# Filter matmuls of both frequency units side by side, six set-up buffers, a separate piece order for the ends, and a new order in the full ticks

## Chip, cores, metric

One core of one Trainium2 chip. The metric is the time of one execution in microseconds (us) of device time; medians of 3 to 7 executions. All executions quoted here were in the same (fast) state, at a mean granted TensorE clock of 0.97 to 0.99. The rounds of experiments ran on different chips; the kernel before, timed again in each, gave medians of 5686.9 to 5687.9 us. PE is TensorE's matmul stream, PEld its weight loads, DVE VectorE, ACT ScalarE, POOL GpSimd, SP SyncE (which only issues transfers here).

## The reference, cut to what matters

Two layers of a MetaFormer block on `x` of 8 x 128 x 128 x 96. Per layer and image:

```python
x_pre = soa(einsum('bhwc,mc->bhwm', ln(x), w1))            # 96 -> 192 channels
xf    = rfft2(x_pre)                                       # 128 x 65 frequencies
comb  = einsum('shwm,bsm->bhwm', filt, softmax(gate(x)))   # 3 resized filters, mixed per image
x     = x + einsum('bhwm,cm->bhwc', irfft2(xf * comb), w2)
t     = x.reshape(B, H * W, C)
x     = t + qlinear(relu(qlinear(q(ln(t)), W1)), W2)       # fp8 products, f16 roundings
```

The Fourier transforms are matmuls with constant matrices. The filters are small (48 rows) and are resized on the fly by a matmul with `k_rh`.

## The kernel before, where the change touches it

The kernel runs as three Python generators, cut at each `yield`: `pixels` (P: a group of 8 image rows through normalisation, `w1` and the first transform), `frequencies` (F: 4 of the 65 columns through filter, second transform, product and inverse) and `tokens` (S: last inverse transform and the fp8 network), plus `gate` (G, once per image) and small normalisation steps (N). A table fixes in which order their pieces are issued in one **tick**; F runs 18 groups behind P and S 38 behind. So there are five phases: set-up, pixels only, pixels and frequencies, some 218 full ticks, frequencies and tokens, tokens only.

```python
TICK = (                       # (stage, piece, groups ahead), 70 entries
    ("S", 22, -2), ("G", 0, -1), ("P", 1, 2), ("F", 2, 0), ("S", 2, 2), ("F", 13, -1),
    ("F", 3, 0), ("P", 3, 1), ("G", 1, -1), ("S", 0, 3), ("N", 0, 0), ("P", 5, 0), ...
)
...
        groups = [[(0, 2)], [(2, 2)] + [(4, 1)] * (n > KC)]
        for units in groups:                      # a unit: two columns, 384 channels
            for j, u in units:
                pf = bank2("pf")                  # one of four PSUM tiles
                ...  mm(pf[...], utf[64*i : 64*i+NHS, ...], kt["rh"][64*i : 64*i+NHS, :])  # 12 matmuls, 48 rows
                py = bank2("py")
                ...  mm(py[...], alf[...], kt["fwd"][:, e, :])                             # 12 matmuls, 128 rows
            yield
            ...  nc.scalar.copy(cv, pf[...])      # cf, ACT
            yield
            ...  products pr = py * cf            # DVE
            yield
            ...  xf = pr[0] + pr[1]               # POOL
            yield
...
        for h in range(2):                        # xn_c: 8 fp8 normalisations per token group
            for j in range(RH * h, RH * h + RH):
                if h in NORM_ACT:  nc.scalar.activation(xn[:, j, :], ...)      # NORM_ACT = ()
                else:              nc.vector.tensor_scalar(xn[:, j, :], ...)
            yield
...     # per third k of the network: y (ACT) -> a (DVE) -> h (POOL) ; at the end y = x + o (POOL)
```

Set-up: all constants on SP's queue, then all filters `cw` (8 loads, 3.7 MB) from POOL's queue, then each layer's small loads; then `u_d` (the half-resized filters, 24 tiles of 65 x 8 x 192) is written from a ring of three buffers.

## Time and profile before

| | before |
|---|---|
| median of 3 | 5689.54 us (5685.1 to 5690.01) |
| first pixel transposes (end of set-up) | 120.2 us |
| pixels only, to the first `pf` | 164.4 us |
| pixels and frequencies, to the first `ps_r` | 301.0 us |
| full ticks, to the last `pa` | 4570.8 us |
| frequencies and tokens, to the last `pi` | 303.0 us |
| tokens only and last stores | 224.8 us |

The phases are read from PE's timeline at the first or last record of the tile named. Lines of the profile are shown in the prediction.

### The profile page before, as it was taken

Reading aid. Unit: us, or ns where it says so; the run is one execution under the profiler, and the core shown is the slowest. Engines: PE = TensorE matmul, PEld = TensorE weight load, DVE = VectorE, ACT = ScalarE, POOL = GpSimd, SP = SyncE. Lnnn points to the kernel's source line nnn. Section 1 sums busy time; section 2 is a strip of 40 time slices with the busy share of each in tenths; the row PEclk is TensorE's granted clock in tenths of the full one; section 3 lists DMA queues with packets and bytes.
Section 4 is the critical chain, followed back from the end, with each engine's and each line's share of the span. In section 5 each row is a group of like instructions: output and inputs, shape, how many; then the busy total and the mean of one; then the engine's idle time right before and its main releaser. Section 6 shows DMA issues by size and latency. Waiting matters only on the chain.

```text
span 5684.2 us, 111449 instructions
## 1 busy us (share of the span) xinstructions
PE 5416.2 (95%) x39144; PEld 4252.6 (75%) x39144; DVE 4387.5 (77%) x11780; ACT 3059.9 (54%) x4575; POOL 4063.1 (71%) x6309
## 2 busy tenths in 40 slices
PE   4899999999999999999999999999999999999876
PEld 1687877878787787878778787877878788787753
DVE  3666787787878778787887878778787877778875
ACT  2444555555555555555555555555555555554444
POOL 1565677777777777777777777777777777777876
PEclk9999999999999999999999999999999999999986
DMA  5465767767676676767667676776767677675642
GB/s 140 145 171 151 198 183 189 196 179 195 179 194 187 187 194 176 195 180 196 185 186 195 180 193 180 194 192 181 195 178 195 178 193 196 178 195 161 169 123 94
DMA packets 830267, 1019.78 MB, mean 179 GB/s; under 512 B 54891, under 2 KB 762203, under 8 KB 829371
## 3 DMA queue, kind: packets, MB, share of 16 engines
q1 hardware_dynamic: 829324, 1008.82, 65.6%
q8 instruction: 312, 5.11, 0.4%
q0 software_dynamic: 384, 3.83, 0.3%
q14 instruction: 247, 2.02, 0.1%
HBM read 598.62 MB, written 413.84 MB: 178 GB/s over the span
## 4 chain that ended last, share of the span: by engine, by line
PE 82%; DVE 7%; POOL 5%; issue 1%; ACT 0%; POOLq 0%; DVEq 0%; ACTq 0%
PE pw L404 13%; PE py L544 13%; PE pa L424 11%; PE pf L533 7%; PE pz L605 7%; PE pz L600 6%; PE pi L619 5%; PE ps_r L649 5%; PE pm L691 5%; PE po L708 4%; PE pt_a L393 4%; DVE xn_c L673 2%; PE pt_c L681 2%; POOL h L703 1%; POOL y L722 1%
## 5 line engine op out<-in xcount | busy, mean ns | idle before, releaser
L703 POOL CAST h<-a 128x1024 fp8e5<-128x1024 f16 x768 | 842.3, 1099 | 962.4 <-DVE a L697 958.0
L411 DVE TENSOR_TENSOR xs<-pw,r 128x768 f32<-128x768 f32 x512 | 489.6, 956 | 766.8 <-ACT r L407 766.8
L582 POOL TENSOR_TENSOR xf<-pr 128x768 f32<-128x768 f32 (+2 forms) x544 | 949.7, 1748 | 67.4 <-DVE pr L574 63.3
L404 PE MATMUL pw<-w,xT 97*128 97x240 f32 x4096 | 921.8, 369 | 5.2 <-DVE yt L626 4.4
L544 PE MATMUL py<-k_fwd,al 128*128 128x128 f32 x6272 | 848.2, 284 | 1.5 <-ACT cf L559 1.2
L404 PEld LDWEIGHTS pw<-w,xT 97*128 97x128 f32 x4096 | 759.5, 191 | 85.7 <-DVE yt L626 11.3
L424 PE MATMUL pa<-xs,dft 128*128 128x384 f32 x2048 | 767.1, 497 | 30.9 <-DVE xs L411 19.1
L544 PEld LDWEIGHTS py<-k_fwd,al 128*128 128x128 f32 x6272 | 740.0, 191 | 73.1 <-issue 5.5
L694 ACT CAST y<-pm 128x1024 f16<-128x1024 f32 x768 | 777.6, 1016 | 1.2 <-PE pm L691 1.1
L559 ACT COPY cf<-pf 128x768 f32<-128x768 f32 (+2 forms) x544 | 419.6, 775 | 536.5 <-PE pf L533 521.7
L673 DVE TENSOR_SCALAR xn_c<-xr,n_rs,n_nb 128x96 fp8e5<-128x96 f32 x2048 | 634.4, 378 | 18.0 <-POOL n_nb L355 16.5
L407 ACT ACTIVATE r<-pw 128x960 f32<-128x960 f32 x512 | 497.0, 971 | 280.9 <-PE pw L404 140.9
L570 DVE TENSOR_TENSOR pr<-py,cf 128x768 f32<-128x768 f32 (+2 forms) x544 | 497.5, 915 | 176.0 <-PE py L544 142.9
L533 PEld LDWEIGHTS pf<-k_rh,ut 48*128 48x128 f32 x6272 | 390.5, 186 | 279.2 <-issue 143.5
L600 PE MATMUL pz<-w2b,xf 128*128 128x192 f32 (+1 forms) x2112 | 551.8, 343 | 27.1 <-POOL xf L582 24.0
L424 PEld LDWEIGHTS pa<-xs,dft 128*128 128x128 f32 x2048 | 367.7, 191 | 224.2 <-DVE xs L411 36.2
L533 PE MATMUL pf<-k_rh,ut 48*128 48x128 f32 x6272 | 494.3, 289 | 1.7 <-DVE pr L574 1.7
L615 ACT COPY zt<-pz 128x384 f32<-128x384 f32 x528 | 251.5, 476 | 448.9 <-PE pz L605 448.5
L600 PEld LDWEIGHTS pz<-w2b,xf 128*128 128x128 f32 (+1 forms) x2112 | 341.3, 191 | 190.6 <-issue 77.6
L691 PE MATMUL pm<-xq,f_q 96*128 96x512 fp8e5 x1536 | 475.7, 393 | 7.5 <-ACT o L717 7.4
L396 ACT ACTIVATE xT<-pt_a 96x1024 f32<-96x1024 f32 x256 | 261.4, 1021 | 395.7 <-PE pt_a L393 395.7
L514 POOL TENSOR_TENSOR ut<-ut,rw 112x768 f32<-112x768 f32 (+1 forms) x256 | 471.6, 1842 | 0.0
(125 smaller groups left out, 10386.8 us busy)
## 6 DMA issues: line engine op xcount, KB each, us to landing
a_d<-at SPq DMA_DIRECT2D x256, 768.0 KB
al<-a_d SPq DMA_DIRECT2D x960, 192.0 KB
v<-y_d SPq DMA_DIRECT2D x256, 384.0 KB
y_d<-yt SPq DMA_DIRECT2D x480, 192.0 KB
ut<-u_d SPq DMA_DIRECT2D x240, 336.0 KB
xt<-in_x_dram SPq DMA_DIRECT2D x128, 384.0 KB
xr<-in_x_dram SPq DMA_DIRECT2D x128, 384.0 KB
mid<-y SPq DMA_DIRECT2D x128, 384.0 KB
```

What stands on the lines that cost most here:

```text
L404: mm(o, xT[:, s * RH + i + j, :], wt["w1"], start=True, stop=True)
L407: nc.scalar.activation(r.rearrange("p s j c -> p s (j c)"), pw, AF.Relu)
L424: mm(pa[:, s], wt["dft"], xss[i // 2][:, s], start=True, stop=True)
L533: mm(pf[:nm, i, t * 128 : (t + 1) * 128], utf[64 * i : 64 * i + NHS, c0 : c0 + nm], kt["rh"][64 * i : 64 * i + NHS, :], start=True, stop=True,
L544: mm(py[:nm, t, e, :], alf[:, e, c0 : c0 + nm], kt["fwd"][:, e, :], start=True, stop=True,)
L570: nc.vector.tensor_tensor(p0, yq, crb, ALU.mult)
L582: nc.gpsimd.tensor_tensor(xv[:q, te], pr[:q, 0, te].rearrange("p t r k -> p t (r k)"), pr[:q, 1, te].rearrange("p t r k -> p t (r k)"), AL ...
L600: mm(o[:, : u * C], xf[:kb, 1, e, :], wt["w2b"][:kb, : u * C], start=True, stop=False,)
L673: nc.vector.tensor_scalar(xn[:, j, :], x8[:, j, :], nm.rs[:, 1, j : j + 1], nm.nb[:, 1, j : j + 1], ALU.mult, ALU.add, saturate=False,)
L691: mm(pm[:, s, :], fk, xq[:, s, :], start=True, stop=True)
L694: nc.scalar.copy(y16, pm)
L703: nc.gpsimd.tensor_copy(hk, a16, saturate=False)
```

## The change

Intent: visit the filter matmuls once per tick instead of twice; give the stretches with only pixels or only tokens an order of their own (`SOLO`); take four of eight `xn_c` of the last image from DVE to ACT; spread the gate; let the set-up begin earlier.

```diff
+TAIL_ACT = (1,)
 TICK = (
-    ("S", 22, -2), ("G", 0, -1), ("P", 1, 2), ("F", 2, 0), ("S", 2, 2), ...
+    ("P", 17, -1), ("F", 13, -1), ("F", 14, -1), ("S", 2, 2), ("S", 18, -1), ("F", 2, 0), ...
+    ... ("G", 0, 0) and ("G", 1, 0) late in the tick before, ("G", 2, -1) to ("G", 6, -1) spread
+SOLO = ( ... P, S and N pieces only ... )
-            nc.gpsimd.dma_start(cw[...], p["cw"][...])
+            nc.sync.dma_start(cw[...], p["cw"][...])
-            u = us.tile([NKW, UN, M], F32, name="u", bufs=3)
+            u = us.tile([NKW, UN, M], F32, name="u", bufs=6)
+    constants("dft", "rw")                       # first; the other constants after the filters
+        for l, p in enumerate(layers):
+            wts.append(prepare(us, l, p))        # small loads of a layer, then its filters
+            cws.append(load_filters(us, l, p))
+        constants("fwd", "inv", "idft", "rh", "mask")
-        for units in groups: ... pf, py / cf / products / xf per unit
+        pf0, pf1 = filter_mm(0, 2), filter_mm(2, 2)
+        yield
+        py0 = fft_mm(0, 2)
+        yield
+        cf0, cf1 = filter_out(2, pf0), filter_out(2, pf1)
+        ...                                      # products, xf, py1 (+ the fifth column), products, xf
-                if h in NORM_ACT:
+                if h in NORM_ACT or (h in TAIL_ACT and jb.n == len(jobs) - 1):
+            alone = t < offset["F"] - 2 or t > n + offset["F"]
+            for stage, step, ahead in SOLO if alone else TICK:
```

## The prediction

> **What bounds the kernel now.** I read the page first: busy shares, the 40 slices, the chain of work that ended last.
>
> ```profile
> PE 5416.2 (95%) x39144; PEld 4252.6 (75%) x39144; DVE 4387.5 (77%) x11780; ACT 3059.9 (54%) x4575; POOL 4063.1 (71%) x6309
> PE   4899999999999999999999999999999999999876
> PEclk9999999999999999999999999999999999999986
> PE 82%; DVE 7%; POOL 5%; issue 1%; ACT 0%; POOLq 0%; DVEq 0%; ACTq 0%
> ```
>
> TensorE (PE) sets the pace from slice 2 to slice 36; only the first 2 and the last 3 or 4 slices (142 us each) show PE idle. The whole idle time of PE is 5684 - 5416 = 268 us, so if "busy" meant "useful" there would be little to win in the middle. So I went to the timeline of PE in one steady tick (a tick: one group of pixels, one of frequencies, one of tokens). `ps_r` comes once a tick, so its starts give the period: 1994.34 to 2014.44 is 20.10 us, and 13 of the 16 ticks of an image have just that.
>
> ```profile
> 1994.34 1.48 PE L649 MATMUL ps_r<-v,k_idft 128*128 128x384 f32 x4
> ...
> 2000.56 1.46 PE L619 MATMUL pi<-zt,k_inv 128*128 128x384 f32 x4
> 2001.94 0.94 PE L533 MATMUL pf<-k_rh,ut 48*128 48x128 f32 x12
> 2002.81 1.60 PE L544 MATMUL py<-k_fwd,al 128*128 128x128 f32 x12
> 2004.25 1.18 PE L708 MATMUL po<-f_q,h 128*128 128x96 fp8e5 x24
> ...
> 2014.44 1.48 PE L649 MATMUL ps_r<-v,k_idft 128*128 128x384 f32 x4
> ```
>
> Read starts, not durations (ends are modelled). The 4 `pi` records take 2000.56 to 2001.94 = 1.38 us, though records of that width follow each other every 0.322 us (4 x 0.322 = 1.29): 0.09 lost before `pf`. The 12 `pf` records take 0.87; in the narrowed timeline they start in pairs 0.112 apart, so 6 x 0.112 = 0.67: 0.20 lost, half at the first pair and half after the last. The 12 `py` take 1.44 against 12 x 0.112 = 1.34: 0.10 lost at the first. One visit to the filter matmuls so costs 0.09 + 0.20 + 0.10 = **0.39 us of PE time counted as busy**, twice a tick. The weight-load row shows the same hole, idle just before the visit:
>
> ```profile
> 2001.94 0.75 PEld L533 LDWEIGHTS pf<-k_rh,ut 48*128 48x128 f32 x12 [0.55 <-ACT n_std L343]
> ```
>
> Adding up the other departures from each record's usual spacing in that tick gives 0.4 us, so a steady tick is PE-issue-bound with almost no waits. The exceptions are the two ticks per image with the gate:
>
> ```profile
> 1821.45 1.48 PE L649 MATMUL ps_r<-v,k_idft 128*128 128x384 f32 x4
> ...
> 1833.70 0.90 PE L465 MATMUL pl<-fc,hb 36*112 36x384 f32 x2 [1.29 <-DVE xs L411]
> ...
> 1835.71 1.65 PE L708 MATMUL po<-f_q,h 128*128 128x96 fp8e5 x24 [0.79 <-ACT lg L470]
> ...
> 1845.93 1.53 PE L424 MATMUL pa<-xs,dft 128*128 128x384 f32 x4 [0.97 <-DVE xs L411]
> ...
> 1848.81 1.48 PE L649 MATMUL ps_r<-v,k_idft 128*128 128x384 f32 x4
> ...
> 1873.42 1.48 PE L649 MATMUL ps_r<-v,k_idft 128*128 128x384 f32 x4
> ```
>
> They last 27.36 and 24.61 us, 11.8 above two plain ticks. Some 4 us of that are real PE work (gate matmuls, the fifth column of the last frequency group); from the spacings I count 5.7 us of waits on VectorE (DVE), which has 11 us of gate arithmetic there. Outside the full ticks, three stretches where PE waits:
>
> ```profile
> 204.88 3.18 PE L424 MATMUL pa<-xs,dft 128*128 128x384 f32 x8 [0.48 <-DVE xs L411]
> 5230.50 0.59 PE L600 MATMUL pz<-w2b,xf 128*128 128x192 f32 x2 [1.69 <-POOL xf L582]
> L703 POOL CAST h<-a 128x1024 fp8e5<-128x1024 f16 x46 | 49.9, 1101 | 34.4 <-DVE a L697 33.2
> ```
>
> They are a pixels-only tick (period 8.03, 1.3 of it waits), a tick of frequencies and tokens alone (mean 15.95 us, PE waits for GpSimd's `xf`), and the tokens-only end (period 10.93; GpSimd itself sits idle 2.2 us per tick for `a`, clock granted 0.67).
>
> **What the Trainium skill says.** "TensorEngine Tiling (Array Packing)", Key Properties: "Changing tiling mode (not just tile) drains the TensorE". `pf` alone in the steady tick contracts over 48 rows in two row groups; everything else uses the full height. The trace agrees, with 0.39 us per visit. "TensorE: Matmul & The Clock Gate", Part 2 step 1: weight loads are pulled ahead of running matmuls; it agrees, loads run ahead everywhere but at these borders. "Trainium Kernel Development and Optimization", Reading a trace, calls matmul busy time a bad metric: agreed, the drain hides inside a PE that is 99% busy between 2000 and 3000 us. "DMA: Bandwidth & Descriptors", on why a DMA increments its semaphore by 16: a transfer is spread over the largest number of engines up to 16 that divides its slowest dimension; 65 partitions give 13 of 16, 81%. The trace agrees: while the `u` tiles are written (56 to 104 us) the DMA share is 0.78 at 212 GB/s.
>
> **The change part by part.** The counts of instructions on all engines stay, except that 64 normalisations go from DVE to ACT and 8 filter loads from GpSimd's to SyncE's queue.
>
> 1. *Filter matmuls together.* Both units' `pf` now stand back to back, then `py`. One visit less in each of 256 frequency ticks (the last group of an image goes from 3 visits to 2). 256 x 0.39 = 100 us; of these 238 ticks are PE-bound now (the other 18 are in item 5): **93 us**. The cost is that two PSUM tiles of four are held at once. I followed the slots through the new order by hand: `pf` takes slots freed by the last `pm` and by `ps_r`; `py1` needs the slot that the first products free, some 1.7 us ahead; `pw1` to `xs` to `pa1` has some 1.4 us. No wait should appear. A plain tick: 20.10 - 0.39 = 19.7, perhaps 19.5.
>
> 2. *Gate in the full ticks.* Gate steps 0 and 1 move into the tick before, the rest is spread. DVE's 16 us per tick plus the 11 are still more than one tick holds, so not all waits go: I take 3 of 5.7, times 15 images: **45 us**.
>
> 3. *Own order for pixels only.* `pw` of the next group now stands between the two `pa`, so `xs` has time. PE floor by spacing: `pt_a` 8 x 0.109, `pw` 16 x 0.202, `pa` 8 x 0.322, together 6.7 us; I take 6.8. 17 ticks x (8.03 - 6.8) = **21 us**.
>
> 4. *Set-up.* First pixel transposes at 120 us. The `u` and padding writes, 24 x 390 KB + 2 x 780 KB = 10.9 MB at 212 GB/s, are 51 us and already fill the 13 engines, so **six buffers alone should give nothing**. But the first write leaves at 55.8; the constants and the first layer's small loads stood behind 3.7 MB of filters (one issue took 16.55 us). In the new order the issues alone (about 0.5 us each, some 60) end near 36 us. First write near 38: **17 us**.
>
> 5. *Frequencies and tokens alone.* The new tick puts both `pf` and the first products early, so `xf` is ready sooner. GpSimd then bounds: 3 casts x 1.1, 2 `xf` x 1.81, `ut` 1.82, `y` 1.64, and 12 small norms x 0.28: 13.7 us. I take 14.3 of 15.95: 17 x 1.6 = **27 us**.
>
> 6. *Tokens only.* GpSimd again: 3.3 + 1.64 + 3.4 = 8.3 us of work per 10.93. With the new order and four normalisations per tick on ACT (about 6 us busy, an estimate from its rows) I take 8.9: 17 x 2.0 = **34 us**.
>
> Sum: 93 + 45 + 21 + 17 + 27 + 34 = 237 us; 5689.5 - 237 = 5452, say 5450.
>
> **The rivals.** *PSUM pressure takes it back:* two `pf` held until ACT has read both leave two slots, and a steady tick gets a new wait of 0.4 us or more. For: four slots, in-order engines, DVE at 80% in the tick. Against: the hand count above. It would leave about 5540. *DVE becomes the bound in the gate ticks:* two such ticks hold 43 us of DVE work against 44 of PE; if the new place only moves the waits, item 2 is zero and the time 5495. *The drain does not disappear with grouping,* because each switch between row groups costs it: against it, pairs inside `pf` already alternate 7 ns apart; it would give 5545. *Only the ends gain:* items 3 to 6 alone, 5590. *Better than thought:* all gate waits go, tick 19.5, end ticks at their floors: 5380.
>
> **Range and chances.** Item 1 is the surest and alone about 1.6%; items 2, 5 and 6 (106 us) I hold to within half. So 5395 to 5510. Under 2% needs over half of the sum to fail (over 5576): faster 0.95, same 0.04, slower 0.01.
>
> **What would show it.** The period of `ps_r` at 19.7 or a little less, and one visit to `pf` of 24 records per tick, with its lost 0.39 once; the two gate ticks together near 48 us instead of 52; pixels-only period 6.8; tokens-only 8.9 with GpSimd's wait for `a` gone; first transposes near 103 us with the same 212 GB/s while `u` is written. It is wrong if the tick stays at 20.1, or `pf`, `py1` or `pa` show idle time before them in a plain tick.

## The result and the profile after

**5454.01 us** (5453.05 to 5458.97, 4 runs) against 5689.77 of before: ratio 0.9589, 95% interval 0.9572 to 0.9606. Ratios here are the mean time of one kernel's fast runs over that of the other's of the same rounds, so not quite the ratio of the medians quoted. The sum of the prediction held, but its terms did not all hold:

| phase | before | after | won | predicted (items) |
|---|---|---|---|---|
| set-up | 120.2 | 115.4 | 4.8 | 17 (4) |
| pixels only | 164.4 | 136.5 | 27.9 | 21 (3) |
| pixels and frequencies, and full ticks | 4871.8 | 4696.3 | 175.5 | 138 (1, 2) |
| frequencies and tokens | 303.0 | 295.9 | 7.1 | 27 (5) |
| tokens only and last stores | 224.8 | 208.1 | 16.7 | 34 (6) |

The profile page of the kernel after: busy shares and the chain that ended last.

```profile
PE 5231.9 (96%) x39144; PEld 4283.1 (79%) x39144; DVE 4371.0 (80%) x11716; ACT 3081.5 (57%) x4639; POOL 4168.3 (76%) x6301
PE 86%; POOL 5%; DVE 4%; DMA 2%; issue 2%; ACT 1%; SPq 1%; POOLq 0%; DVEq 0%; ACTq 0%
```

PE's "busy" fell by 184 us with the same 39144 matmuls, so that much of it had not been needed for them (the grouping alone, the second run below, takes 67 us of it: 5349.3 busy). The share rose by one point only, so the share does not show it. A steady tick, PE's timeline after (start, duration, engine, line, tile):

```profile
1875.82 1.45 PE L686 MATMUL ps_r<-v,k_idft 128*128 128x384 f32 x4
1877.11 0.49 PE L637 MATMUL pz<-w2b,xf 128*128 128x192 f32 x2
...
1878.72 1.61 PE L553 MATMUL pf<-k_rh,ut 48*128 48x128 f32 x24
1880.26 1.60 PE L566 MATMUL py<-k_fwd,al 128*128 128x128 f32 x12
...
1884.19 1.46 PE L656 MATMUL pi<-zt,k_inv 128*128 128x384 f32 x4
1885.49 1.50 PE L566 MATMUL py<-k_fwd,al 128*128 128x128 f32 x12
...
1895.37 1.45 PE L686 MATMUL ps_r<-v,k_idft 128*128 128x384 f32 x4
```

Period 1895.37 - 1875.82 = **19.55** (20.10 before). The 24 `pf` take 1880.26 - 1878.72 = 1.54 us where 12 + 12 took 1.74; `pi`, no longer ahead of a filter visit, takes 1.30 instead of 1.38. The three ticks around the gate begin at:

```profile
786.52 1.45 PE L686 MATMUL ps_r<-v,k_idft 128*128 128x384 f32 x4
...
810.24 1.45 PE L686 MATMUL ps_r<-v,k_idft 128*128 128x384 f32 x4
...
831.66 1.45 PE L686 MATMUL ps_r<-v,k_idft 128*128 128x384 f32 x4
```

The ticks are 23.23 (up to the first of these), 23.72 and 21.43: 9.7 above three plain ticks, in some images 9.0; before 27.36 + 24.61 + 20.42, 12.1 above. There are 13 such groups in the full ticks; of the 16 gates the first falls into pixels only, the second into pixels and frequencies, the last into frequencies and tokens. Pixels only:

```profile
202.59 1.04 PE L412 MATMUL pt_a<-ident,xn_a 128*96 128x128 f32 x8
...
209.29 1.04 PE L412 MATMUL pt_a<-ident,xn_a 128*96 128x128 f32 x8
```

Period 6.70 (8.03 before), with no wait: the floor that I had worked out. The two late stretches, where less came: PE's wait for `xf` with frequencies and tokens (period 15.55, in the mean 15.94 before; the wait was 1.69), and POOL's casts in the tokens-only end (groups of 5260 to 5412 us, period 10.1):

```profile
5081.49 0.59 PE L637 MATMUL pz<-w2b,xf 128*128 128x192 f32 x2 [1.60 <-POOL xf L596]
```

```profile
L740 POOL CAST h<-a 128x1024 fp8e5<-128x1024 f16 x46 | 49.7, 1096 | 19.6 <-DVE a L734 19.6
```

POOL still waits for `a`: 0.43 us a cast instead of 0.75. In the set-up, SP's queue shows where the early start was lost (start, time of the issue):

```profile
17.21 6.03 SPq L219 DMA_DIRECT2D bet<-in_L_conv_bn_beta_dram  x1
23.28 6.23 SPq L219 DMA_DIRECT2D bmu<-in_L_conv_bn_mean_dram  x1
...
52.26 20.52 SPq L211 DMA_DIRECT2D u_d<-u  x12
```

Two small loads, issued right behind a layer's filters, hold the queue for 12 us; the first `u` leaves at 52.3, not near 38.

### The profile page after: what moved, and what is told of

Its sections match the earlier page's. It is cut to its first block, busy times and chain, and to the rows that moved or that the text cites.

```text
span 5452.2 us, 112019 instructions
## 1 busy us (share of the span) xinstructions
PE 5231.9 (96%) x39144; PEld 4283.1 (79%) x39144; DVE 4371.0 (80%) x11716; ACT 3081.5 (57%) x4639; POOL 4168.3 (76%) x6301
## 4 chain that ended last, share of the span: by engine, by line
PE 86%; POOL 5%; DVE 4%; DMA 2%; issue 2%; ACT 1%; SPq 1%; POOLq 0%; DVEq 0%; ACTq 0%
PE pw L423 15%; PE py L566 13%; PE pa L443 12%; PE pz L642 7%; PE pf L553 7%; PE pz L637 6%; PE pi L656 6%; PE ps_r L686 5%; PE pm L728 5%; PE po L745 4%; PE pt_a L412 4%; DVE xn_c L710 2%; PE pt_c L718 2%; POOL h L740 1%; DMA u_d<-u 1%
## 5 line engine op out<-in xcount | busy, mean ns | idle before, releaser
L740 POOL CAST h<-a 128x1024 fp8e5<-128x1024 f16 x768 | 802.0, 1047 | 629.1 <-DVE a L734 626.0
L596 POOL TENSOR_TENSOR xf<-pr 128x768 f32<-128x768 f32 (+2 forms) x544 | 994.4, 1830 | 213.6 <-DVE pr L588 211.5
L566 PEld LDWEIGHTS py<-k_fwd,al 128*128 128x128 f32 x6272 | 760.9, 191 | 116.6 <-issue 11.7
L566 PE MATMUL py<-k_fwd,al 128*128 128x128 f32 x6272 | 821.3, 280 | 4.8 <-ACT cf L573 3.0
L734 DVE TENSOR_SCALAR a<-y,b 128x1024 f16<-128x1024 f16 x768 | 429.7, 565 | 189.3 <-ACT y L731 155.4
L710 DVE TENSOR_SCALAR xn_c<-xr,n_rs,n_nb 128x96 fp8e5<-128x96 f32 x1984 | 552.8, 351 | 35.1 <-POOL n_nb L374 35.0
L637 PE MATMUL pz<-w2b,xf 128*128 128x192 f32 (+1 forms) x2112 | 535.5, 335 | 24.2 <-POOL xf L596 24.0
L637 PEld LDWEIGHTS pz<-w2b,xf 128*128 128x128 f32 (+1 forms) x2112 | 355.5, 191 | 161.4 <-POOL xf L596 33.9
L754 ACT CAST o<-po 128x768 f16<-128x768 f32 x256 | 204.5, 799 | 469.3 <-PE po L745 469.3
L573 ACT COPY cf<-pf 128x768 f32<-128x768 f32 (+2 forms) x544 | 394.5, 776 | 122.9 <-PE pf L553 120.2
```

What stands on the lines that cost most here:

```text
L566: mm(py[:nm, t, e, :], alf[:, e, cs], kt["fwd"][:, e, :], start=True, stop=True)
L596: nc.gpsimd.tensor_tensor(xv[:q, te], pr[:q, 0, te].rearrange("p t r k -> p t (r k)"), pr[:q, 1, te].rearrange("p t r k -> p t (r k)"), AL ...
L637: mm(o[:, : u * C], xf[:kb, 1, e, :], wt["w2b"][:kb, : u * C], start=True, stop=False,)
L710: nc.vector.tensor_scalar(xn[:, j, :], x8[:, j, :], nm.rs[:, 1, j : j + 1], nm.nb[:, 1, j : j + 1], ALU.mult, ALU.add, saturate=False,)
L740: nc.gpsimd.tensor_copy(hk, a16, saturate=False)
```

## The experiments

Theories: *drain* (a visit to the 48-row matmuls costs 0.39 us, nothing else in them does); for the set-up, *engines* (13 of 16 bound the `u` writes) against *issue* (time lost before the first write); for the ends, *GpSimd as bound* against something that delays what GpSimd waits for. Each kernel was correct. "After" means the changed kernel at 5454.

**Two visits again, the rest as after.**

```diff
-        pf0, pf1 = filter_mm(0, 2), filter_mm(2, 2)
+        pf0 = filter_mm(0, 2)
         yield
         py0 = fft_mm(0, 2)
+        pf1 = filter_mm(2, 2)
```

> The changed kernel with the second pair's filter matmuls put after the first FFT matmuls again (two visits to the 48-row mode per tick), everything else as changed. Drain theory: the steady tick grows from 19.55 by 0.39 to 19.94 us and the time by 0.39 x 256 = 100 us to about 5554 us. Rival (the new order of pieces alone made the steady tick shorter, the visits cost nothing): the tick stays at 19.55 and the time at 5454 us.

5644.89 us, ratio to before 0.9925: 191 of the 236 us are gone, twice what the drain alone predicts. The plain tick is 20.38, +0.83. PE's timeline of it:

```profile
1988.17 0.94 PE L553 MATMUL pf<-k_rh,ut 48*128 48x128 f32 x12
...
1990.58 0.94 PE L553 MATMUL pf<-k_rh,ut 48*128 48x128 f32 x12
...
1992.79 1.86 PE L423 MATMUL pw<-w,xT 97*128 97x240 f32 x8 [0.26 <-DVE pr L588]
```

The first `pf` to `pw` (`py` and `pt_a` left out above) takes 4.62 us here; in the kernel after the same matmuls take 3.85. The rest has two parts. `pw` waits for a PSUM tile that DVE's products free later now. The line shows 0.26 us idle, but ends are modelled: by starts, in a narrower window, the last `pt_a` begins at 1992.25 and `pw` at 1992.79, 0.53 apart where `pt_a` records otherwise follow each other in 0.11, so the wait costs about 0.43. The 0.40 left of the 0.83 is what a visit was said to cost. In a kernel with four PSUM tiles the move of a matmul group changes two things, its own cost and which slot it gets, and this run shows both; the next has the cost alone in its plain tick.

**Only the grouping, in the old order** (in the kernel before: both `pf`, then `py0`; both `cf` copies together; nothing else).

```diff
             if units[0][0] == 0:
+                for j, u in ((0, 2), (2, 2)):
+                    pfs[j] = filter_mm(j, u)          # both, ahead of py
-            ... cf of this unit
+            early[j] = filter_out(u, pfs[j])          # both copies at once
```

> The kernel before with only the filter matmuls of both units put together (and their copies on ScalarE), in the old order of pieces and the old set-up. Drain theory without new waits: the steady tick goes from 20.10 to 19.71 us, the time from 5690 to about 5590 us. Rival (two more PSUM tiles held make new waits in the old order, which the new order was needed to avoid): the tick stays at 20.1 or grows, the time is 5690 us or more.

5619.72 us, ratio 0.9879. Plain tick:

```profile
1963.74 1.48 PE L664 MATMUL ps_r<-v,k_idft 128*128 128x384 f32 x4
1965.16 1.61 PE L533 MATMUL pf<-k_rh,ut 48*128 48x128 f32 x24
...
1983.45 1.48 PE L664 MATMUL ps_r<-v,k_idft 128*128 128x384 f32 x4
```

19.71 us, 0.39 less, to the hundredth. The two phases where PE bounds won 84.7 + 5.6 = 90 us (item 1 said 93). But frequencies and tokens alone became 21.8 us longer (324.8). I did not separate the grouped matmuls from the grouped copies there; POOL's first `xf` of a tick now waits 1.2 us for DVE's products. Grouping without a new order gives part back; that the whole gain is kept is the new order's doing. The gate ticks are about 12 us above three plain ones, as before: grouping does nothing for them.

**Three buffers instead of six.**

```diff
-            u = us.tile([NKW, UN, M], F32, name="u", bufs=6)
+            u = us.tile([NKW, UN, M], F32, name="u", bufs=3)
```

> The changed kernel with three u buffers in the set-up in place of six. Theory (the u writes already fill the 13 DMA engines that a 65-partition tile gets): the first pixel transposes stay at 115 us within 2 us, and the time at 5454 us within 3. Rival (the buffers are what shortened the set-up): the transposes move to 120 us or later.

5457.19 us, ratio 0.9592; first transposes at 116.4 (115.4). Six buffers do nothing that can be measured, as predicted. The reason given was wrong, which the next run shows.

**All sixteen transfer engines for `u`** (each write of 65 partitions split in 64 + 1).

```diff
-            nc.sync.dma_start(u_d[l][:, n1 : n1 + UN, :], u)
+            for k0, k1 in ((0, 64), (64, NKW)):
+                nc.sync.dma_start(u_d[l][k0:k1, n1 : n1 + UN, :], u[k0:k1])
```

> The changed kernel with each u tile and the padding written in two DMAs, of 64 partitions and of 1, in place of one of 65. If the writes are bound by 13 of 16 engines, the 10.9 MB need 51 x 13/16 = 41 us: the first pixel transposes come about 8 to 10 us earlier, at 106 us, and the DMA share while u is written rises from 0.77 towards 0.9. Rival (bound by HBM or by the producers): no change, 115 us.

5456.52 us, ratio 0.9593; first transposes 116.4. The stretch 56 to 96 us of the kernel after, then of this one (last two columns: share of the transfer engines' time, GB/s):

```profile
56.00:96.00 40.00, 26.61 (x128) 7.88 (x128) 18.32 (x36) 15.35 (x36) 0.00 (x0) 0.50 0.79 227
```

```profile
56.00:96.00 40.00, 27.57 (x128) 7.98 (x128) 18.32 (x36) 15.32 (x36) 0.00 (x0) 0.50 0.98 213
```

All engines are now busy, and no more is moved: a packet of 6144 bytes takes 0.47 us in the median instead of 0.23. A busy share of 13/16 was not the bound. What does bound these writes at 210 to 230 GB/s stays open; no run changed the number of partitions that a write reads from.

**Filters from another queue.**

```diff
-            nc.sync.dma_start(cw[...], p["cw"][...])
+            nc.scalar.dma_start(cw[...], p["cw"][...])
```

> The changed kernel with the filters (cw) loaded over ScalarE's DMA queue in place of SyncE's. Theory (the set-up gained 5 us in place of 17 because two small loads of the second layer stood 6 us each behind the filters in SyncE's queue, and the constants 2.6 us each behind the second filters): the first u write leaves near 35 us in place of 49 to 52, the first pixel transposes come at 100 to 104 us in place of 115, the time is about 5442. Rival (the loads share the same DMA engines, so only the place of the wait moves): 115 us, 5454.

5448.84 us, ratio 0.9581; first transposes 108.2. SP's queue:

```profile
18.81 0.54 SPq L219 DMA_DIRECT2D bet<-in_L_conv_bn_beta_dram  x1
19.40 1.35 SPq L219 DMA_DIRECT2D bmu<-in_L_conv_bn_mean_dram  x1
...
48.82 43.78 SPq L211 DMA_DIRECT2D u_d<-u  x24
```

The two loads cost 0.5 and 1.4 us instead of 6.0 and 6.2, and the set-up is 7.2 us shorter. But this run does not show that the shared queue was the cause. ACT issues the filters here one or two at a time, and from 16 to 22 us none is in flight: all 1411 packets of that stretch are under 2 KB, while a filter's have 18432 bytes. In the kernel before, the filters came over another queue too, POOL's, and the same load of the first layer was held longest of all:

```profile
4.71 16.55 SPq L203 DMA_DIRECT2D bet<-in_L_conv_bn_beta_dram  x1
```

The next (`bmu`) took 6.15 and was let go at 27.5; the last large filter packets start before 26 us. So the record fits a hold by filters in flight, over whichever queue they come, and not the order in one queue; no run isolates it, and why just these two loads are held so long was not tested. The other part of the missing 12 us is not the loads: the issues end at 39.9 now, and the first `u` still leaves at 48.8, because PE's `ps_u` starts at 43.0 (37.2 after). So the expectation of 100 to 104 was half right.

**One order everywhere** (no `SOLO`).

```diff
-            for stage, step, ahead in SOLO if alone else TICK:
+            for stage, step, ahead in TICK:
```

> The changed kernel with the order of the full ticks used everywhere, so without the own order where only pixels or only tokens are left. Theory (the own order gives the pixels-only period of 6.70 us, bound by TensorE, and the tokens-only 10.1): pixels-only goes back to about 8.0 us (+22 us over 17 ticks), tokens-only to between 10.1 and 10.9; in all +20 to +36 us, about 5480. Rival (the new tick order alone did it): no change, 5454 us.

5483.18 us, ratio 0.9642. Pixels only is back at 8.01 us per tick (20.8 us longer), tokens only 7.1 us longer (10.57 per tick). So the own order is worth 20.8 us in pixels only (item 3 said 21). The other 7 us that this phase won remain without it. They lie where the first image's gate falls: by the starts of `pt_a`, the last two ticks before the first `pf` are 8.03 + 19.32 us in the kernel before and 8.51 + 9.42 here (2.6 of these 9.4 us go again, as `pf` comes later in its tick).

**The gate in one tick, new order.**

```diff
-    ... ("G", 0, 0) ... ("G", 1, 0) in the tick before, ("G", 2, -1) ... ("G", 6, -1) spread
+    ... ("G", 0, -1) to ("G", 6, -1), all in one tick
```

> The changed kernel with the seven gate steps packed into one tick again, as far as can be beside the same pieces as in the kernel before; the rest of the tick's order as changed. Theory (spreading the gate is worth about 3 us per image): the three ticks around it last 59.4 + 9 = 68.4 us now, and would go to 71 or more; in all +35 to +60 us, about 5500. Rival (gate waits shrank because the tick has other slack): 5454 us, within 10. The plain tick stays at 19.55 us in both.

5568.43 us, ratio 0.9793 (interval 0.9777 to 0.9809: at 2%, unclear against before). The plain tick stays 19.55; the gate ticks are 30.54 + 23.23 + 21.44, 16.6 above three plain ones (9.7 or 9.0 after). The full ticks lose 94.8 us, 7.3 for each of their 13 gates, more than the 35 to 60 expected in all; with the gates of the other phases (4 us more in pixels only, 9 in pixels and frequencies, 4 in frequencies and tokens) it is 112 of the run's 114. So where the gate stands is worth as much as the grouping in this tighter tick; PE waits for `xs` from DVE, as the prediction's 5.7 us of waits had it for the kernel before. A part of this is not waiting: two gate operations of DVE on 36 x 1 elements (`hm`) last 1.52 and 2.13 us before, 0.29 and 2.14 here, 0.21 and 0.15 after; the runs on `xn_c` below show a delay of the same kind.

**Half of `xn_c` on ACT as soon as no pixels are left** (not only in the last image).

```diff
-                if h in NORM_ACT or (h in TAIL_ACT and jb.n == len(jobs) - 1):
+                if h in NORM_ACT or (h in TAIL_ACT and late[0]):      # late[0] = t > n, set per tick
```

> The changed kernel with half of the token normalisations on ScalarE from the tick after the last pixels on, in place of only for the last image. In the ticks of frequencies and tokens a ring is seen: GpSimd's n_nb, then eight xn_c on VectorE (4.2 us), then a, then GpSimd's h. Theory (that ring sets the 15.55 us): four xn_c less on VectorE take about 1.5 to 2 us out, the period goes to about 13.9 and the time to 5454 - 17 x 1.6 = 5427 us. Rival (another wait ends there, xf before pz): 15.5 us, no change.

5437.60 us, ratio 0.9562; period 15.55 to 14.59 (13.9 expected), the phase 15.7 us shorter. This is most of the missing part of item 5. DVE and POOL of one tick, first the kernel after:

```profile
5079.71 4.21 DVE L710 TENSOR_SCALAR xn_c<-xr,n_rs,n_nb 128x96 fp8e5<-128x96 f32 x8 [1.23 <-POOL n_nb L374]
```

```profile
5079.63 1.80 POOL L596 TENSOR_TENSOR xf<-pr 128x768 f32<-128x768 f32 x1
5081.38 1.04 POOL L740 CAST h<-a 128x1024 fp8e5<-128x1024 f16 x1
5084.38 2.21 POOL L740 CAST h<-a 128x1024 fp8e5<-128x1024 f16 x2 [1.96 <-DVE a L734]
```

then with half on ACT:

```profile
5087.13 3.25 DVE L710 TENSOR_SCALAR xn_c<-xr,n_rs,n_nb 128x96 fp8e5<-128x96 f32 x4 [1.23 <-POOL n_nb L374]
```

```profile
5090.84 2.21 POOL L740 CAST h<-a 128x1024 fp8e5<-128x1024 f16 x2 [1.00 <-DVE a L734]
```

The four `xn_c` that stay are not four times 0.32 us. In the single records the first begins 0.08 us after POOL's `xf` and lasts 1.79, as long as `xf` (1.80); the second begins beside `h` and lasts 1.06 (`h`: 1.04); the last two, with POOL waiting, last 0.32. In the kernel after, `xn_c` beside `xf` lasts 1.79 in the median of some 18, alone 0.32. The Trainium skill, "SBUF — State Buffer", Who interferes with whom, says that VectorE and GpSimd share a pair of ports under an exclusive lock, that `tensor_scalar` can take it, and that the second one "fully blocks" until the first is done. The trace agrees, with these numbers. So DVE is held by POOL, `a` comes late, and POOL then waits for `a` (1.96 us, now 1.00): each engine is the other's delay.

**All of `xn_c` on ACT.**

```diff
-TAIL_ACT = (1,)
+TAIL_ACT = (0, 1)                                # and late[0] as above
```

> As e7, but all eight token normalisations on ScalarE from the tick after the last pixels on. In e7 the first two xn_c of a tick last 1.79 and 1.06 us, as long as the xf and h that GpSimd runs beside them (1.80, 1.04), and 0.32 alone. Theory (VectorE is held out by GpSimd, so that the ring GpSimd n_nb, xn_c, a, h stays long whatever the number of xn_c on VectorE): with none left there the ring is open, GpSimd's own 13.7 us bound, the period goes from 14.59 to 13.7 to 13.9 and the time from 5438 to about 5425 us. Rival (the ring is only long by the number of instructions, or the eight on ScalarE delay y and xq as much): 14.6 us or more, 5438 or more.

5441.66 us, ratio 0.9568; period 14.66. The rival was right: eight `xn_c` in a row hold ACT for 2.97 us, the third `y` comes behind them, and POOL again waits 1.01 us for `a`. Item 5's 14.3 is not reached either way; 13.7 is further off still.

**Another order of the tokens-only end** (with the half on ACT).

```diff
-    ("P", 2, 1), ("S", 4, 1), ("S", 17, -1), ... ("S", 22, -2), ("S", 2, 2), ... ("S", 0, 3), ... ("S", 3, 2), ...
+    ("P", 2, 1), ("S", 17, -1), ("S", 3, 1), ("S", 4, 1), ... ("S", 0, 3), ("S", 22, -2), ("S", 2, 2), ...
-        xr = ab.tile([128, 2, RH, C], F32, name="xr", bufs=5)
+        xr = ab.tile([128, 2, RH, C], F32, name="xr", bufs=6)
```

> As e7, with a changed order for tokens only: the normalisations after the last a of the group before, and the load of v and xr ahead of the store of y (one more xr buffer). Theory (two rings of 10.1 us there: GpSimd y, SyncE's queue, load of v, ps_r, add, norms; and n_nb, xn_c, a, h): the tokens-only period goes from 10.1 to about 8.8, GpSimd's work of 8.5 us, 22 us less than e7: 5416. Rival (the loads come from HBM too late anyhow, or ScalarE's chain bounds): 10 us, 5438. The ticks with frequencies stay at 14.59.

5465.61 us, ratio 0.9609: tokens-only went from 10.1 to 12.01 us. DVE and POOL:

```profile
5340.67 3.13 DVE L748 TENSOR_SCALAR xn_c<-xr,n_rs,n_nb 128x96 fp8e5<-128x96 f32 x4
```

```profile
5341.85 1.63 POOL L797 TENSOR_TENSOR y<-xr,o 128x768 f32<-128x768 f32 x1
...
5346.15 0.21 POOL L389 TENSOR_TENSOR n_d<-st 128x8 f32<-128x8 f32 x1 [2.66 <-DVE st L369]
```

I had moved `xn_c` beside `h` and `y` of POOL. Four of them take 3.13 us (alone 1.3); the statistics `st` come late, and POOL stands for 2.66 us.

**Everything together**: that order, all of `xn_c` on ACT, filters on ACT's queue (the three diffs above).

> The changed kernel with e8 (filters over ScalarE's queue), e9 and e10 together. If the parts add up: 5454 - 8 - 29 - 22 = 5395 us. If ScalarE becomes the bound in the tokens-only ticks (3 y, xq, o, 8 normalisations: about 8.3 us, an estimate from its rows in the changed kernel), 5400 to 5410. Rival (the parts hide one another): 5420 or more.

**5421.96 us** (5420.77 to 5423.96), ratio 0.9534, interval 0.9519 to 0.9548: faster than both kernels, about 32 us below the change, but 27 above the 5395 expected for parts that add up; the rival's "5420 or more" came true. The tokens-only period is 9.3 on average. Against the run before it only `xn_c` differs in this phase: with none on DVE the same order turns from 12.01 to 9.3. That is the plainest test of the lock-out here. Half on ACT with frequencies and all in the tokens-only end was not run; from this phase's length in the two runs (280.3 with half, 283.5 with all) an estimate is some 3 us more.

**No `xn_c` on ACT, the rest as after.**

```diff
-TAIL_ACT = (1,)
+TAIL_ACT = ()
```

> The kernel after, but the 64 normalisations of the last image that it gives to ACT stay on DVE (the tuple of halves that go to ACT is empty). Nothing else differs, so every phase but tokens-only must be equal to within 1 us. If the normalisations on DVE beside GpSimd work are what holds the tokens-only end (lock-out theory): eight of them run there instead of four, each some 0.8 us instead of 0.3 while GpSimd casts, so 3 us more DVE time per tick, about half of it seen: period 10.1 to 11.5, 17 ticks x 1.4 = 24 us slower, about 5478. Rival: the own order alone made the gain of the tokens-only end, and four normalisations more on DVE (4 x 0.3 = 1.2 us beside an engine that is not the bound) cost nothing: 5454, period 10.1. Note that the order alone was worth 0.45 per tick in the run with one order.

5463.31 us, ratio 0.9605; tokens-only 10.9 per tick, the phase 12.2 us longer, all others equal to within 0.8. It lies between the two expectations. One `xn_c` of each four is held to 1.00 or 1.04 us by a cast (the others 0.32), not all eight as I had put it. With the new order but all on DVE the end takes as long per tick as before (10.93), and the phase is only 4.5 us shorter: the own order pays there mostly together with the move to ACT.

## Why the prediction was right, and where its steps failed

The time (5450 predicted, 5454) and the direction are right, and the mechanism that carries it, the drain, is shown. But the miss of 4 us is luck in part: three steps promised 49 us too much, two 44 us too little.

- **Item 1, grouping: right.** 0.39 us a visit, read from three gaps between starts, is what the old order with grouped filters shows (20.10 to 19.71), and 90 us for 93.
- **Item 2, gate: near in size, by a wrong count.** "Times 15 images" failed: the full ticks hold 13 gates. There 12.1 went to about 9.3 us above plain ticks, some 36 us. The second image's gate brought some 10 us more with pixels and frequencies (the 18.1 won there less 20 ticks of 0.40), the first image's the 7 us above: together some 53 for 45. Not all waits went, as said.
- **What items 1 and 2 left out:** the new order by itself takes another 0.15 us off a plain full tick (19.71 to 19.55; some 218 ticks, 34 us). The prediction saw 0.4 us of other departures from the usual spacings in a steady tick ("perhaps 19.5") but put nothing for it into the sum. The starts show where most of it lay: the four `ps_r` take 1.42 us up to the next start where `pf` follows them (1963.74 to 1965.16, grouping only) and 1.29 where `pz` does (1875.82 to 1877.11, after), and a `pm` pair ahead of `pz` takes 0.48 against 0.44. With pixels and frequencies, where no `ps_r` runs, the plain tick is 15.46 us in both orders.
- **Item 3, pixels only: right,** 6.70 for 6.8 per tick and 20.8 us for 21 by the own order; the floor by spacing was reached. The phase won 7 us more, from the first image's gate, which is not in the sum.
- **Item 4, set-up: wrong in size, 5 for 17.** The failed step is "the issues alone (about 0.5 us each, some 60) end near 36 us": while the first layer's filters are in flight two issues of the second layer take 6 us each. A warning stood in the kernel before: I quoted an issue of 16.55 us, as one that "stood behind" the filters, though these were in another queue, and assumed that no such thing would be left in the new order. That 13 engines are filled and so bound the writes is wrong too; with all 16 the same bytes take as long.
- **Item 5, frequencies and tokens: wrong in size, 7 for 27.** The failed step is "GpSimd then bounds", a sum of durations on one engine. POOL is not busy all the time; it waits for `a`, and `a` waits because DVE's `xn_c` is locked out while POOL works. Moving them gave 15.7 us of the missing 20.
- **Item 6, tokens only: wrong in size, 17 for 34.** "GpSimd's wait for `a` gone" failed: it fell from 0.75 to 0.43 us a cast, since four `xn_c` stayed on DVE. With none there and a matching order the period is 9.3; 8.9 was not reached by any run.
- **Rivals.** PSUM pressure did not come in the new order, though two visits in that order do show such a wait (0.43 us a tick by starts): the hand count was needed. "Only the ends gain" is refuted: they gave 57 of 232 us, the ticks the rest.

## What to carry to other kernels

Read a pipelined engine's starts, not its busy share: 184 us of "busy" TensorE time vanished here with the same matmuls, 67 of them with the grouping alone, which takes away two borders per tick between 48-row and full-height matmuls. A bound made by adding up one engine's durations holds only if nothing of another engine that shares its ports stands between; for VectorE and GpSimd look at whether the same operation is long beside the other and short alone, and if so move it to ScalarE. When a group of matmuls is moved in a kernel with few PSUM tiles, expect the slots to move too, and test the cost by itself in the old order.

## What the Trainium skill lacked or had wrong

- "TensorEngine Tiling (Array Packing)", Key Properties, names the drain but not its price: 0.39 us per visit to 48-row matmuls amid full-height ones (20.10 to 19.71 us a tick when one visit goes), and none between the pairs inside a visit.
- "DMA: Bandwidth & Descriptors", on why a DMA increments its semaphore by 16: k = 13 of 16 for 65 partitions is right in the trace (share 0.79, with all 16 0.98), but a reader may take the smaller k for a bandwidth loss, as I did: 227 against 213 GB/s, packets 0.23 against 0.47 us.
- I found no page with the time that the issue of a small load is held while large transfers are in flight: 6.03 and 6.23 us with the filters in the same queue, 16.55 and 6.15 with the filters in another (the kernel before), 0.54 and 1.35 with none in flight.
- "SBUF — State Buffer", Who interferes with whom, was right and would have mended items 5 and 6: `xn_c` 1.79 us beside GpSimd's `xf`, 0.32 alone. Small operations suffer as well: in the kernel before, the gate's two operations on 36 x 1 elements (`hm`) lasted 1.52 and 2.13 us beside GpSimd's work on 768 elements a row and more.
